# A four-layer vision kernel: one more filtered position in the second 3x3 convolution, middle outputs summed by accumulating transfers, one map buffer instead of two

## The chip, the cores and the metric

The kernel runs on one core of one Trainium2 chip. The metric is the device time of one execution in microseconds; every number here is from executions on the chip. A core has TensorE (PE, with its weight loads as PEld), VectorE (DVE), ScalarE (ACT), GpSimd (POOL), SyncE (SP), and 16 DMA engines that move data for queues which SP, ACT and POOL issue to.

## The reference

A tensor x of 4 images, 256 channels, 56 x 56, float32, passes four residual layers. Each normalizes x in 32 groups (`_gn`) and adds a branch:

```python
x = x + _L0_conv_ref(_gn(x), ...)   # involution 7x7, 16 groups
x = x + _L1_conv_ref(_gn(x), ...)   # two 3x3 convolutions
x = x + _L2_conv_ref(_gn(x), ...)   # involution 7x7 with batch norms
x = x + _L3_conv_ref(_gn(x), ...)   # spectral gates

def _L1_conv_ref(x, w1, g1, b1, rm1, rv1, w2, g2, b2, rm2, rv2):
    h = _conv3x3(x, w1, stride=1)
    h = jax.nn.relu(_bn(h, g1, b1, rm1, rv1))
    h = _bn(_conv3x3(h, w2, stride=1), g2, b2, rm2, rv2)
    return jax.nn.relu(x + h)
```

The change is in layer 1, the two 3x3 convolutions from 256 to 256 channels.

## The kernel before, in words

The layers run one after the other: the first involution up to about 517 us of the span, the convolution layer up to about 1166, then the second involution with the gates. Everything on an engine runs in the order in which the program emits it (`in_order` pins it), so a wait of one instruction holds all behind it on its engine.

`conv_layer` cuts each image into three chunks of rows, 12 chunks in all: 18, 20, 18 rows for the first convolution (`C1_ROWS`) and 16, 20, 20 for the second (`C2_ROWS`). The order is first 0, first 1, second 0, first 2, second 1, first 3, second 2, and so on; second 10 is followed by second 11. The output map of the first convolution is kept in `ph2`, which has two halves used in turn (`i % 2`).

Along a row both convolutions use a minimal-filtering transform: four outputs are computed from six products, the positions k, done in the order `KS = (1, 2, 3, 4, 0, 5)`. `transform` (L1414 to L1455, nine steps, VectorE, and one ACT copy of known rows, L1417) makes the six inputs v from a map; `input1` and `input2` are the two instances. VectorE then combines the six products into four outputs.

A position is done in one of two ways. *Unfiltered* (`unfiltered`, L1525): for each half `co` of the outputs, 6 products (3 rows x 2 halves of inputs) over the whole chunk. *Filtered* (`filtered_product`, L1540): a second transform along the column gives two outputs from four products over half the rows. For that it needs the columns' sums and differences of the input, `inner_columns` (L1491, L1492, VectorE) and `outer_columns` (ACT L1507, then an accumulating transfer by POOL, L1508), and transformed weights: the sum and the difference of three weight rows (`column_sums_of`, L1318 to L1320, VectorE) and scalings on ACT. Of a filtered position's four products, ACT copies the first from PSUM (L1549) and VectorE does three sums (L1550, L1551, L1553). Before the change, filtering is used for all six positions of first convolutions from chunk 2 on, five in chunk 1, none in chunk 0, and for positions 4 and 0 of all second convolutions. Each product of two float32 operands is two PE instructions in the trace.

PSUM is four tiles of two banks, used in turn (`two_banks`). A filtered position takes two tiles, an unfiltered one takes one.

Everything else is placed by hand into twelve lists `after[0]` to `after[11]` for every convolution: items of `after[2n]` are emitted inside the n-th position in `KS` order, those of `after[2n+1]` behind it. The text calls them slots. `place(after, g, at)` puts the steps of a generator g into the slots `at`. `late_r[k]` is a list for slot k of the *next* convolution (k of 12 and more is the one after that). `tail1` holds what the first convolution leaves to the next: the ACT passes `outputs` (L1570) that write `ph2`. `phases` (L1411, ACT) normalizes the next rows of x.

For chunks up to 9, `joined` hands the second convolution's outputs on: ACT writes the output scaled (L1652), a POOL transfer adds x (L1653), ACT applies the relu (L1660), a POOL transfer adds x again (L1661), SP stores the result (L1663), and ACT makes the sums for the next normalization (`mean_of` L1691, `spread_of` L1697, L1698). Chunks 10 and 11 load x (`load_residual`) and join on VectorE (L1670, L1675); chunk 10 adds x by a POOL transfer (L1685) and stores by POOL (L1686). `weights2` (`summed_weights`) forms the second convolution's weights by accumulating transfers from DRAM (L1298) during the first two chunks.

## Time and profile before

| | |
|---|---|
| median of 3 runs | 1714.48 us (1708.15 to 1714.85) |
| the profiled execution | 1717.23 us, its span 1715.5 us |
| busy, share of the span | PE 95%, PEld 85%, DVE 78%, ACT 58%, POOL 29% |
| L1525, unfiltered products | 1320 instructions, 295.1 us of PE |
| L1540, filtered products with all operands | 2848 instructions; the two largest groups 175.9 and 73.5 us |
| PE idle in the layer, largest waits | 7.6 us (a transfer into u_sb), 3.0 (DVE L1553), 2.9 (DVE L1608) |
| DMA queues, share of 16 engines | POOL's 24.8%, SP's 29.9% |

Busy times say how long an engine was executing; what an edit is worth follows from which engine ends last in the stage where it lies. Lengths of single matmuls overlap, so the cost of one is the distance between starts. An idle time in brackets stands before the instruction, with what ended it.

### The profile page before, as it was taken

The numbers are of one execution on the slowest core, as the hardware profiler recorded it, in microseconds if no ns is written. First come the engines' busy times: TensorE is split into PE (matmuls) and PEld (weight loads), VectorE is DVE, ScalarE is ACT, GpSimd is POOL, SyncE is SP. The second block draws the span as 40 slices with busy tenths as digits, with TensorE's granted clock in tenths as the row PEclk, the third lists the DMA queues.
The fourth block names the chain that finished last, engine by engine and source line by source line (L and its number), as shares of the span: only waits on it lengthen the run. The fifth ranks groups of instructions, "written<-read, shape, count | busy, mean of one in ns | idle before, by whom it ended". The sixth has DMA issues, their size and how long they took to land.

```text
span 1715.5 us, 57009 instructions
## 1 busy us (share of the span) xinstructions
PE 1632.9 (95%) x24488; PEld 1466.1 (85%) x24488; DVE 1333.8 (78%) x2439; ACT 1000.9 (58%) x2192; POOL 498.2 (29%) x711
## 2 busy tenths in 40 slices
PE   6999999999989999999999999988999999899988
PEld 4998998988987889899999889976988888788876
DVE  2687787777759998999889899947777778778775
ACT  1655556456545565565666456435667567577654
POOL 2124223322433222212212212110000572572571
PEclk9999999999999999999999999999999999999996
DMA  2354445433759666566766556644444765764762
GB/s 90 114 184 138 147 147 185 154 127 104 238 139 281 112 129 106 121 129 138 148 132 113 109 122 128 142 132 147 129 139 162 207 215 184 218 210 140 204 169 98
DMA packets 92490, 258.63 MB, mean 151 GB/s; under 512 B 14837, under 2 KB 37374, under 8 KB 88526
## 3 DMA queue, kind: packets, MB, share of 16 engines
q1 hardware_dynamic: 57438, 163.33, 29.9%
q0 software_dynamic: 33760, 90.37, 24.8%
q8 instruction: 194, 3.18, 0.8%
q10 hardware_dynamic: 1040, 1.26, 0.3%
q14 instruction: 58, 0.48, 0.1%
HBM read 95.07 MB, written 49.15 MB: 84 GB/s over the span
## 4 chain that ended last, share of the span: by engine, by line
PE 64%; DVE 15%; DMA 7%; issue 5%; ACT 3%; SPq 2%; POOL 2%; ACTq 0%; POOLq 0%; DVEq 0%
PE mm L1540 17%; PE ps L594 15%; PE ps L636 13%; PE mm L1525 11%; DVE kt L612 5%; DMA xw<-xw 4%; PE ps L408 3%; DVE un L656 3%; DMA u_sb<-in_wc_dram 2%; PE ps L470 1%; SPq L426 1%; SPq L427 1%; DVE st L1106 1%; ACT hp L489 1%; ACT xw L420 1%
## 5 line engine op out<-in xcount | busy, mean ns | idle before, releaser
L636 PE MATMUL ps<-kt,xw 126*32 126x48 f32 (+1 forms) x12544 | 381.7, 236 | 24.1 <-DMA xw<-xw 11.3
L636 PEld LDWEIGHTS ps<-kt,xw 126*32 126x32 f32 (+1 forms) x12544 | 343.0, 122 | 69.7 <-issue 44.0
L594 PE MATMUL ps<-hp,z_sb 64*126 64x133 f32 x6144 | 384.3, 279 | 9.0 <-DVE kt L612 4.9
L594 PEld LDWEIGHTS ps<-hp,z_sb 64*126 64x126 f32 x6144 | 364.4, 185 | 25.0 <-DVE kt L612 6.9
L612 DVE TENSOR_TENSOR kt<-ps,zb_sb 126x798 f32<-126x798 f32 x352 | 332.9, 980 | 59.3 <-PE ps L594 47.9
L605 ACT ACTIVATE kt<-ps,zb_sb 126x133 f32<-126x133 f32 x960 | 281.0, 442 | 107.3 <-PE ps L594 107.3
L1525 PE MATMUL mm<-v,u_sb 128*128 128x280 f32 (+2 forms) x1320 | 295.1, 383 | 1.7 <-DVE xs L1551 1.0
L1525 PEld LDWEIGHTS mm<-v,u_sb 128*128 128x128 f32 x1320 | 247.5, 189 | 41.8 <-issue 1.6
L1540 PE MATMUL mm<-xs,u_sb 128*128 128x126 f32 (+2 forms) x1392 | 175.9, 279 | 0.3 <-DVE xs L1551 0.3
L656 DVE SCALAR_TENSOR_TENSOR un<-ps,s,un 128x240 f32<-128x240 f32 x224 | 102.5, 457 | 89.0 <-ACT un L651 83.7
L1540 PEld LDWEIGHTS mm<-xs,u_sb 128*128 128x128 f32 x1392 | 168.5, 193 | 0.5 <-issue 0.5
L656 DVE SCALAR_TENSOR_TENSOR un<-ps,par_sb,un 128x240 f32<-128x240 f32 x224 | 97.6, 456 | 81.8 <-ACT un L649 77.9
L1508 POOL DMA_DIRECT2D xs<-v x82 | 75.2, 1006 | 285.3 <-ACT xs L1507 233.9
L661 POOL TENSOR_TENSOR xs<-un,xs 128x240 f32<-128x240 f32 x112 | 72.2, 665 | 216.3 <-DVE un L656 216.3
L420 ACT COPY xw<-ps 126x896 f32<-126x896 f32 x112 | 101.4, 906 | 39.0 <-PE ps L408 21.3
L649 ACT ACTIVATE un<-ps,par_sb 128x240 f32<-128x240 f32 x112 | 50.3, 449 | 119.1 <-PE ps L636 112.8
L151 POOL TENSOR_TENSOR norm_sb<-norm_sb,mhalf 128x1 f32<-128x1 f32 x32 | 19.8, 642 | 342.5 <-DVE norm_sb L150 342.5
L651 ACT ACTIVATE un<-ps,bn_t,s 128x240 f32<-128x240 f32 x112 | 60.1, 538 | 94.2 <-PE ps L636 86.0
L408 PE MATMUL ps<-ident_sb,strip_sb 128*126 128x128 f32 x784 | 110.6, 281 | 3.9 <-ACT hp L489 1.6
L408 PEld LDWEIGHTS ps<-ident_sb,strip_sb 128*126 128x126 f32 x784 | 84.0, 141 | 15.0 <-POOL strip_sb L393 4.6
L1411 ACT ACTIVATE ph<-xs,norm_sb 128x266 f32<-128x266 f32 (+2 forms) x96 | 80.4, 862 | 9.0 <-DMA xs<-x 7.3
L1540 PE MATMUL mm<-v_sb,u_sb 128*128 128x140 f32 (+2 forms) x536 | 73.5, 280 | 3.5 <-DVE xs L1553 3.0
(303 smaller groups left out, 2272.7 us busy)
## 6 DMA issues: line engine op xcount, KB each, us to landing
xw<-xw SPq DMA_DIRECT2D x224, 252.0 KB
xw<-xw SPq DMA_DIRECT2D x224, 126.0 KB
xs<-x POOLq DMA_DIRECT2D x26, 560.0 KB, 5.9
x<-xs POOLq DMA_DIRECT2D x8, 1568.0 KB, 7.8
xs<-x SPq DMA_DIRECT2D x8, 1568.0 KB
xs<-v POOLq DMA_DIRECT2D x42, 252.0 KB, 4.3
xs<-in_x_dram SPq DMA_DIRECT2D x6, 1568.0 KB
x<-xs SPq DMA_DIRECT2D x6, 1568.0 KB
```

Source lines behind the costliest of these rows:

```text
L408: nc.tensor.transpose(ps[:Q, k * P : (k + 1) * P], flat[:, k * Q : (k + 1) * Q], ident_sb)
L420: nc.scalar.copy(xw[:, :NSB, :], ps[:Q, : NSB * P].rearrange("q (n c) -> q n c", n=NSB))
L594: nc.tensor.matmul(ps[:Q, i, k * NT : (k + 1) * NT], z_sb[i * R : (i + 1) * R, cb * GB // 2 + gp, z0 : z0 + Q], hp[i * R : (i + 1) * R, py ...
L605: nc.scalar.activation(kt[:, g0 + i, pb, :, k], ps[:Q, i, k * NT : (k + 1) * NT], AF.Identity, bias=zb_sb[:, cb * GB + g0 + i, p0 + k : p0 ...
L612: nc.vector.tensor_tensor(kt[:, g0 : g0 + 2, pb], ps[:Q, :, : PB * NT].rearrange("q i (k t) -> q i t k", k=PB), zb_sb[:, cb * GB + g0 : cb ...
L636: nc.tensor.matmul(v[m * j : m * j + m, i, :, k * TP : (k + 1) * TP], xw[:, window(ty), m * j : m * j + m], kt[:, ng * j : ng * j + ng, :, ...
L656: nc.vector.scalar_tensor_tensor(part, o[e], s, part, ALU.mult, ALU.add)
L661: nc.gpsimd.tensor_tensor(dst, u, dst, ALU.add)
L1411: nc.scalar.activation(dst, xr[:, j], AF.Identity, bias=t, scale=s)
L1508: nc.gpsimd.dma_start(t[:, at], v[:, at], accum_op=ALU.add)
L1525: nc.tensor.matmul(ps, *position(u, v, ci, dy, k, co, n), start=(j == 0), stop=(j == NB * 3 - 1))
L1540: nc.tensor.matmul(ps[:, bank, co * m : (co + 1) * m], u[ci][:, co * P : (co + 1) * P], v2[:, : n // 2, ci * WT : (ci + 1) * WT], start=(c ...
```

## The change

- Second convolutions filter three positions, 3, 4 and 0, instead of 4 and 0; chunk 1 of the first convolution filters four (1 to 4) instead of five.
- The combination is rearranged. Before, positions 0 and 5 were folded in by scaled sums (`stt`) at the end. Now z and s, the first and the last output, are formed at position 4, and positions 0 and 5 are added onto them (`onto`), in `filtered_product` with a VectorE sum that broadcasts the first product in place of ACT's copy. The transform's sign at L1441 and the weights change with it.
- The two middle outputs get their last sum by `middle`: two POOL transfers that accumulate in SBUF and one ACT halving, in first convolutions from chunk 2 and second ones from 1 to 9; else two VectorE operations as before.
- `ph2` holds one chunk. All four `outputs` passes of a first convolution now stand in slots 0 to 3 of the following second convolution (except chunk 0). Of `input2`'s nine steps eight, not five, lie in the first convolution before. New room: `y_sb`, two more tiles for sums.
- Column sums of the weights used late (second convolution 3, 4, 0; first 0, 5) are made by `edge_column_weights`: ACT copies and scalings with three POOL transfers, for both input halves at once.
- Placement: the first L1652 pass of a chunk moves from the end of its convolution to slot 0 of the next, the second from slot 0 to slot 2; the relu and what follows one slot later. Outer columns of the second convolution stand in slots 0, 1, 2 (before 2 and 3), inner ones in 1 and 3. In the last chunk outer columns are made by one VectorE subtraction each. Chunk 10 stores by SP.

```diff
-                return KS[: (0, 5, 6)[min(i, 2)]]
+                return KS[: (0, 4, 6)[min(i, 2)]]
...
+                    nc.scalar.mul(us[ci][0], us[ci][0], 6.0)
...
-            FILTERED2 = (4, 0)
+            FILTERED2 = (3, 4, 0)
...
+            def edge_column_weights(u, k, x, scratch):
+
+                w0, w1, w2 = (u[:, :, y, k, :] for y in range(3))
+                s = y_tile(scratch)[:, : NB * C].rearrange("p (c n) -> p c n", c=NB)
+                nc.scalar.copy(s, w0)
+                nc.scalar.mul(x, w1, -1.0)
+                yield
+                nc.gpsimd.dma_start(s, w2, accum_op=ALU.add)
+                yield
+                nc.gpsimd.dma_start(x, s, accum_op=ALU.add)
+                nc.gpsimd.dma_start(w1, s, accum_op=ALU.add)
+                yield
+                for w, by in ((w1, 0.5), (x, 0.5), (w2, -1.0)):
                     nc.scalar.mul(w, w, by)
-
-            def filtered2(i):
-
-                return FILTERED2
+                yield
...
-            ph2 = wpool.tile([P, 4, 2 * PH_ROWS, NB, WT + 1], F32, name="ph2")
+            ph2 = wpool.tile([P, 4, PH_ROWS, NB, WT + 1], F32, name="ph2")
...
-                    stt(one(k), d, -4.0, far, ALU.mult, ALU.add)
+                    stt(one(k), d, 4.0, far, ALU.mult, ALU.subtract)
...
-                if (conv, i) == (1, 1):
+                if (conv, i) in ((1, 1), (2, n_chunks - 1)):
                     tt(t[:, at], v[:, at], v[:, below], ALU.subtract)
                 else:
                     nc.scalar.mul(t[:, at], v[:, below], -1.0)
...
-                nc.scalar.copy(o[:, 0], m1)
-                tt(o[:, 1], o[:, 0], m2, ALU.subtract)
-                tt(o[:, 0], o[:, 0], m2, ALU.add)
+                if onto is None:
+                    nc.scalar.copy(o0, m1)
+                    tt(o1, o0, m2, ALU.subtract)
+                else:
+                    tt(o, o, m1.to_broadcast([P, 2, NB * n // 2, WT]), ALU.add)
+                    tt(o1, o1, m2, ALU.subtract)
+                tt(o0, o0, m2, ALU.add)
                 run_all(items)
                 tt(o, o, outer[:, :, : NB * m].rearrange("p e (r t) -> p e r t", t=WT), ALU.add)
 
+            def middle(t, q, b, a, by_transfer):
+
+                if by_transfer:
+                    nc.gpsimd.dma_start(b, a, accum_op=ALU.add)
+                    nc.scalar.mul(t, t, 0.5)
+                    nc.gpsimd.dma_start(t, q, accum_op=ALU.add)
+                else:
+                    tt(b, b, a, ALU.add)
+                    stt(t, t, 0.5, q, ALU.mult, ALU.add)
...
                     elif k == 4:
                         tt(full(b), full(t), got, ALU.add)
                         tt(full(t), full(t), got, ALU.subtract)
-                        tt(b, b, a, ALU.subtract)
-                        stt(t, t, 0.5, q, ALU.mult, ALU.add)
-                    elif k == 0:
-                        stt(full(a), full(a), -0.75, got, ALU.mult, ALU.add)
-                        stt(a, b, 0.25, a, ALU.mult, ALU.add)
-                        outputs(2, 1)
-                    elif k == 5:
-                        stt(full(q), full(q), -3.0, got, ALU.mult, ALU.add)
-                        stt(q, t, 4.0, q, ALU.mult, ALU.add)
+                        stt(z, b, 0.25, a, ALU.mult, ALU.add)
+                        stt(s, t, 2.0, q, ALU.mult, ALU.add)
+                        middle(t, q, b, a, i > 1)
+                        if i == 0:
+                            edge_rows(i)
+                            outputs(2, 1)
                     run_all(after[2 * n_s + 1])
-                tail += [lambda: outputs(0), lambda: outputs(3)]
+                if i == 0:
+                    tail += [lambda: outputs(0), lambda: outputs(3)]
+                else:
+                    tail += [lambda: (edge_rows(i), outputs(0)), lambda: outputs(3), lambda: outputs(2), lambda: outputs(1)]
...
-                        if co == 0:
-                            leaves()
-                        else:
-                            late_r[0].append(leaves)
-                        k = 5 + 2 * co
+                        late_r[2 * co].append(leaves)
+                        k = 6 + 2 * co
...
-                        k = 10 + 2 * co
+                        k = 11 + 2 * co
...
-                    nc.gpsimd.dma_start(xout[bb][co][:, at], x)
+                    nc.sync.dma_start(xout[bb][co][:, at], x)
...
+                        middle(t, q, b, a, 0 < i and summed)
...
-                    stt(q[:, at], q[:, at], -3.0, ps, ALU.mult, ALU.add)
-                    stt(q[:, at], t[:, at], 4.0, q[:, at], ALU.mult, ALU.add)
+                    tt(s[:, at], s[:, at], ps, ALU.add)
...
-                        place(after, late_v, (1, 3, 5, 8, 10))
+                        place(after, late_v, (1, 3, 5, 6, 8, 9, 10, 11))
...
-                                after[0].append(lambda ci=ci: column_weights(ci, 0, 1))
-                                after[1].append(lambda ci=ci: filter_weights(ci, 0, 1))
+                            place(after, edge_column_weights(u2_sb, 3, ux2_sb[0], 6), (4, 5, 8, 11))
+                            fourth = edge_column_weights(u2_sb, 4, ux2_sb[1], 3)
+                            place(after, fourth, (5, 6, 9))
...
-                        place(after, late_v, (0, 0, 1, 1))
+                        place(after, late_v, (0,) if i < n_chunks - 1 else ())
...
+                    after[1].append(lambda i=i: inner_columns(2, i, 3, 4))
+                    after[3].append(lambda i=i: inner_columns(2, i, 0))
+                    for n, k in enumerate(FILTERED2):
+                        after[n].append(lambda i=i, k=k: outer_columns(2, i, k))
                     if i == 0:
...
+                        place(after, fourth, (1,))
+                        place(after, edge_column_weights(u2_sb, 0, ux2_sb[2], 5), (0, 1, 3, 5))
+                        place(after, edge_column_weights(u1_sb, 0, ux0_sb, 4), (3, 4, 6, 9))
+                        place(after, edge_column_weights(u1_sb, 5, ux5_sb, 5), (6, 7, 9, 11))
...
-                        place(after, input1(j), (1, 1, 2, 2, 3, 3, 4, 4, 5))
-                        columns_at(after, (6, 8), ((4, 1), (4, 2), (6, 3), (9, 4)), 1, j)
+                        place(after, input1(j), (1, 2, 2, 3, 3, 4, 5, 6, 7))
+                        columns_at(after, (6, 8, 11), ((4, 1), (5, 2), (7, 3), (9, 4)), 1, j)
                     elif nxt is not None:
-                        place(after, input2(nxt[1]), (1, 1, 2, 2, 3, 3, 4, 5, 6))
+                        place(after, input2(nxt[1]), (4, 4, 5, 5, 6, 6, 7, 8, 9))
```

## The prediction

> **What bounds the kernel now.** I read the page first: TensorE is busy 95% of the span, and its two convolution lines (L1525 unfiltered, L1540 filtered) lead the chain that ended last. Then the timeline of TensorE from one first convolution to the next, for the price of a position. "x24" or "x16" counts instructions; the difference of two starts is the real cost, since each length contains about 0.16 us of pipeline tail.
>
> ```profile
> 707.92 1.12 PE L1540 MATMUL mm<-v_sb,u_sb 128*128 128x140 f32 x8
> ...
> 711.73 5.82 PE L1525 MATMUL mm<-v,u_sb 128*128 128x280 f32 x24
> 717.39 1.12 PE L1540 MATMUL mm<-ph,u_sb 128*128 128x140 f32 x8
> ...
> 757.45 1.06 PE L1540 MATMUL mm<-v_sb,u_sb 128*128 128x112 f32 x8
> ...
> 761.02 4.72 PE L1525 MATMUL mm<-v,u_sb 128*128 128x224 f32 x24
> 765.58 1.05 PE L1540 MATMUL mm<-ph,u_sb 128*128 128x126 f32 x8
> ```
>
> A 20-row chunk pays 711.73-707.92 = 3.81 us for a filtered position and 717.39-711.73 = 5.66 for an unfiltered one: 1.85 saved by filtering. A 16-row chunk pays 3.57 and 4.56: 1.0 saved.
>
> Then the windows view, cut at chunk boundaries (first convolution, second, and again). Columns: length, busy PE, PEld, DVE, ACT, POOL, granted clock, DMA share, GB/s.
>
> ```profile
> 840.30:870.60 30.30, 30.30 (x162) 25.82 (x162) 28.87 (x46) 13.91 (x29) 5.25 (x6) 1.00 0.55 131
> 870.60:893.50 22.90, 22.90 (x194) 22.89 (x193) 18.90 (x35) 17.76 (x25) 5.39 (x8) 1.00 0.74 127
> 893.50:918.80 25.30, 25.30 (x163) 25.29 (x161) 24.79 (x38) 13.26 (x27) 5.22 (x6) 1.00 0.61 148
> ```
>
> TensorE never stops here, but VectorE is 95 to 98% busy in a second convolution (rows one and three) and 83% in a first. So time taken from TensorE comes back only if VectorE and what feeds it keep up.
>
> Last, the waits and the timelines where TensorE does stop: 7.6 us in the last chunk, behind POOL, and some 9 us of idle and slow clock around 555 to 570.
>
> ```profile
> 1151.91 4.07 PE L1540 MATMUL mm<-u_sb 128*128 128x140 f32 x16 [7.59 <-DMA u_sb<-v]
> ```
> ```profile
> 1139.44 0.57 POOL L1686 DMA_DIRECT2D x<-xs  x1 [5.22 <-DMA xs<-x]
> 1140.04 0.86 POOL L1685 DMA_DIRECT2D xs<-x  x1
> 1147.13 0.55 POOL L1686 DMA_DIRECT2D x<-xs  x1 [6.23 <-DMA xs<-x]
> 1147.67 1.76 POOL L1508 DMA_DIRECT2D u_sb<-v  x2
> ```
> ```profile
> 568.05 1.27 POOL L1298 DMA_DIRECT2D u_sb<-u_sb  x1 [0.78 <-DMA u_sb<-in_wc_dram]
> ```
>
> **The end: -12 us.** In the last chunk the outer columns went through ACT and a POOL transfer; POOL sat behind an output store (L1686) that waited for a landing. The change makes these columns on VectorE (0.73 each) and sends that store by SP, so the 7.6 goes. So does the slow clock after it: those 16 instructions took 4.07 where 2.07 is usual. VectorE is busy only 17.6 of this chunk's 40.5 us, so three columns and one more product hide there. Two chunks (10 and 11) save 1.85 each: 7.6+2.0+3.7 = 13.3. Chunk 10 gives back about 1.3: its middle sums stay on VectorE (+1.4) and the next chunk's nine transform steps (8.4 us) move from slots 1-6 to 4-9, behind products; VectorE then ends some 18 us of work against 17.1 of TensorE. Bounds -8 to -14; I take -12, near the plain sum, since the wait is shown. What is late next is VectorE's own tail.
>
> **The start (518 to 612): +4 us.** Removed from VectorE: column sums for first-conv positions 0, 5 and second-conv 4, 0 (24 operations of 0.43, 10 us), inner and outer columns of chunk 1's position 0 (2.0). Chunk 1 then loses its second wait (3.3) and the slow clock behind it (1.8), and pays 1.85 for position 0 unfiltered: its TensorE ends near 581, not 584. But the sums' first step is an ACT copy of position 3's weights at slot 4. Its last accumulation is issued at 568.05 and lands 7.7 later (median of L1298), at 575.8. ACT is in order: behind the copy stand phases (0.8 each), the copies of position 4 and that position's PSUM copy, which reaches VectorE near 580 instead of 568. VectorE then owes 13 us before the inner columns of the second convolution's position 3 exist (594, against TensorE's 590): 4 lost. Each later set of weights is a chain on POOL: ACT copy, transfer (4.3 to land), two transfers (1.0 to issue each, 4.3), three ACT scalings; position 0's is ready near 607, and I count 3 more. Chunk 0 would end near 616 against 612.3: +4. Bounds: -5 (weights early enough) to +10 (also each scaling blocks a PSUM copy and the clock drops).
>
> **The pairs between: -3 us.** TensorE saves 6x1.85+3x1.0 = 14. Per pair VectorE gets +1.6 (three operations of position 3's product), +0.9 (its inner columns), +2.2 (three broadcast sums in place of ACT copies), and loses 2.9+2.35 of scaled sums (L1604 to L1609, L1733 to L1742): -0.5 in all. The two middle sums it sheds are replaced by z and s. So its load stays, in a shorter pair: about 97%. POOL gets four sums and one outer column, 5x1.0; DMA engines 5x1.55 for 280 KB (the windows of 723 to 738 are filled for 15.4 us by the 2.8 MB of L1653, L1508 and L1661): 7.7 us more in 50, hidden, since their share is 0.55 to 0.74.
>
> Moved at no cost: the passes L1652 (2.45 each on ACT) from the end of the second convolution to slots 0 and 2 of the next first, where ACT is 17.8 of 22.9 us busy and gives up four output passes (2.2); the transforms of the next chunk, one slot later each; inner columns 0 and 5 (1.3) into the second convolution's last position, where VectorE else has 1 of 5.7 us. Without that cover each would cost its length. The single map is read last at slot 9 of the first convolution and rewritten from slot 0 of the second, so I expect no wait for it.
>
> What isn't hidden is order. (1) Three transform steps (3.2 us) move into the first convolution, so VectorE ends it 5 us late, not 3 to 4. (2) ACT: four output passes (1.1 each) and two means now stand at the start of the second. After the combinations (19 us into a 20-row first convolution, as L1602 ends now) come the halving on ACT 0.6, two POOL sums 2.0, then L1661, landing in 5.9: 26.5, or 3.6 into the second. Then, in order: mean 1.4, phases 0.75, outputs 1.1, outer column 0.5 (7.3), PSUM copy 0.45, mean 1.4, outputs 1.1, outer 0.5, row copy L1417 0.35 (11.1), outputs 1.1, outer 0.5, square 1.45, outputs 1.1 (15.2), and only then position 3's PSUM copy, which a 16-row chunk has ready at 11.0. L1417 holds VectorE's next transform until 11.1 in two chunks of three. From there VectorE has 17 us up to releasing the PSUM banks that the next first convolution needs: 28.0, where TensorE is done at 24.3 and the chunk takes 25.3 now: +2.7. The same count gives 30.25 against 30.3 for the 20-row chunk with L1417 and about -1.6 for the one without: +1.1 per image. With ACT never late, VectorE alone allows -4.7. The landing may be off by 2 us either way, so I take -1.0 per image, nearer to the count: -3. Bounds -14 and +15 (every chunk 1.2 us worse than counted, with cold clocks).
>
> The granted clock was 0.66 from 565 to 570, after waits of 2.9 and 3.0 us, and the 32 instructions there cost 1.8 us more. That is in the upper bound.
>
> The Trainium skill (TensorE: Matmul & The Clock Gate, "What's actually happening") says that an idle window of about 3.4 us halves the clock; by it the short new waits of 1 to 3 us cost nothing beyond themselves. This trace saw it dip after two shorter ones close together. By the trace's 1.8 us in each of nine chunks the sum would be 16 us worse, by the page none.
>
> The Trainium skill (DMA: Bandwidth & Descriptors, "Anatomy of one DMA") gives 2.0 us plus bytes at 436 GB/s, estimated 2.7 us for 280 KB; the row of L1508 has 4.7 for this accumulation. By the page each sum would land 2 us earlier, the pairs give about -8; the measurement decides.
>
> **Sum.** -12+4-3 = -11. The profiled execution took 1717.23 (span 1715.5, 1.7 around it), 2.7 above the median 1714.48 of three; the same -11 on the median gives 1703.5. 0.5%, 8.6 us, is what a measurement here can tell from none.
>
> **Rivals.** First: everything hides. Weights land in time (-3), ACT never holds VectorE (-14), the end as shown (-13): -30, 1684.5. For it: VectorE's total falls. Against: 97% load, and the means behind a landing.
>
> Second, slower: ACT's queue at the start of a second convolution decides. Each microsecond that position 3's PSUM copy comes later than counted costs each of nine chunks one; 1.2 later takes away the whole gain, 2.2 makes it slower by over 0.5%. At 2.7 later: -11+24 = +13, 1727.5. For it: position 3 is the second-convolution filter closest to the start. Against: ACT is only about half busy in second convolutions.
>
> **Numbers.** Forecast 0.5 (own range 1695 to 1712), first rival 0.25, second 0.25. Faster by over 0.5% (below 1705.9): 0.29 of the forecast's half and 0.24 of the first's, 0.53. Slower (above 1723): 0.19, from the second and its neighbourhood; within: 0.28. The range for 8 in 10 leaves out the outer tenth of each rival's side: 1683 to 1729.
>
> **What would show it.** Right: no wait on u_sb<-v in the last chunk; a second convolution of 16 rows at least as long as 25.3 us, VectorE waiting there for ACT's L1417 or position 3's PSUM copy; ACT waiting for a landing near 565 to 576. The first rival: 20-row pairs near 49.9 us with no TensorE wait. The second: waits of 3 us or more in every second convolution. Wrong altogether: new TensorE waits on transfers, or a changed later layer.

## The result and the profile after

The changed kernel takes 1761.26 us, the median of 4 runs (1757.48 to 1772.66), against 1714.66 before in the same session: a ratio of 1.0285, 95% interval 1.0256 to 1.0314, clearly slower. The forecast was 1703.5 with a range up to 1729. The profiled execution took 1757.48, its span 1755.7; before, 1717.23 and 1715.5.

The layer can be cut into the prediction's three steps, with what lies behind it as a fourth (us; distances between starts of products in the traces). A pair is a first convolution and the second convolution behind it:

| | before | after | predicted | measured |
|---|---|---|---|---|
| start: first product to first convolution 2 | 93.6 | 97.9 | +4 | +4.3 |
| pairs: from there to second convolution 10 | 482.2 | 524.6 | -3 | **+42.4** |
| end: from there to the layer's last product | 71.2 | 65.1 | -12 | -6.1 |
| later layers | 549.7 | 549.7 | 0 | 0.0 |

So one term is wrong by 45 us and one by half. Here are windows of the profile after, the same three chunks that the prediction showed (second convolution 5, first 7, second 6; length, then busy PE, PEld, DVE, ACT, POOL, granted clock, DMA share, GB/s):

```profile
862.37:895.97 33.60, 30.34 (x171) 26.79 (x170) 25.57 (x42) 17.92 (x35) 7.38 (x13) 0.95 0.69 155
895.97:918.89 22.92, 22.92 (x193) 22.92 (x192) 20.70 (x40) 14.37 (x17) 7.98 (x11) 1.00 0.79 136
918.89:951.60 32.71, 27.50 (x171) 27.34 (x170) 24.72 (x42) 16.83 (x35) 7.88 (x10) 0.90 0.71 157
```

The first convolution is unchanged (22.9). The second ones, which should have become shorter, take 33.6 and 32.7 us where they took 30.3 and 25.3. TensorE stops in them, and VectorE is no longer full: 24.7 of 32.7 us, where it was 24.8 of 25.3. Neither is the bound; something holds both. TensorE's timeline in the same chunks says where it stops:

```profile
879.02 3.39 PE L1549 MATMUL mm<-xs,u_sb 128*128 128x140 f32 x16 [3.26 <-DMA xs<-v]
...
935.12 3.73 PE L1549 MATMUL mm<-xs,u_sb 128*128 128x112 f32 x16 [5.21 <-DMA xs<-v]
```

These are the products of position 3's outer column, which ACT's L1516 and POOL's transfer L1517 make (L1507 and L1508 before). They wait for its landing, and the 16 instructions behind then last 3.4 to 3.7 us instead of 2.0: the clock, 0.95 and 0.90 in the windows. The Trainium skill (TensorE: Matmul & The Clock Gate, "What's actually happening") puts the clock's fall at an idle window of about 3.4 us; six waits of 3.26 to 5.81 us here, each with such slow products behind it, agree roughly.

From the list of waits of the profile after, three lines (total, times, longest):

```profile
ACT xs L1709 <- DMA xs<-x: 45.3, 9, 6.0
DVE v L1449 <- ACT v L1425: 29.5, 10, 7.8
PE mm L1549 <- DMA xs<-v: 29.3, 8, 5.8
```

ACT's L1709, the mean of a finished chunk, waits for the second accumulation of x (L1681, L1661 before). ACT runs in order, so behind it stand position 3's outer column, whose lateness stops TensorE, and the known rows L1425, which stop VectorE. Of the eight waits in the third line six are long, 3.3 to 5.8 us, in second convolutions 1, 2, 3, 5, 6 and 8; the other two are 0.67 and 0.25. In those six the mean starts 6.0 to 7.8 us into the chunk. In 4 and 7 it starts after 3.6, and TensorE doesn't wait for the column. The timelines of POOL, SP, ACT, POOL and PE around second convolution 2 (its start is 695.73) show one such chain:

```profile
691.80 0.86 POOL L1572 DMA_DIRECT2D hp<-y_sb  x1 [7.19 <-DVE hp L1623]
693.05 0.86 POOL L1574 DMA_DIRECT2D hp<-xs  x1 [0.39 <-ACT hp L1573]
693.59 1.21 POOL L1681 DMA_DIRECT2D xs<-x  x1
693.57 11.55 SPq L1165 DMA_DIRECT2D xs<-x  x2
702.54 1.14 ACT L1709 ACTIVATE xs<-xs 128x1120 f32<-128x1120 f32 x1 [5.48 <-DMA xs<-x]
705.66 0.65 ACT L1516 ACTIVATE xs<-v 128x560 f32<-128x560 f32 x1
706.61 0.86 POOL L1517 DMA_DIRECT2D xs<-v  x1 [9.88 <-ACT xs L1516]
713.01 3.56 PE L1549 MATMUL mm<-xs,u_sb 128*128 128x140 f32 x16 [3.89 <-DMA xs<-v]
```

L1681 stands in POOL's queue behind the two new middle sums (L1572, L1574), and SP's load of the next rows (L1165) starts beside it. It lands 9.0 us after its issue, 6.8 into the second convolution. The trace's answer for this line says the same of the whole layer. Before (L1661), this is who waited for it, and its landing:

```profile
  ACT xs L1691: 0.2, 1
...
DMA to landing us min/median/max: 5.3/6.6/8.3
```

and after (L1681):

```profile
  ACT xs L1709: 45.3, 9
...
DMA to landing us min/median/max: 6.2/8.9/10.6
```

The end after: no wait on u_sb<-v is left, as predicted, but second convolution 10 begins with a wait, and three more follow around its end, each on VectorE:

```profile
1140.79 11.56 PE L1534 MATMUL mm<-v,u_sb 128*128 128x280 f32 x48 [1.84 <-DVE hp L1565]
...
1171.80 0.35 PE L230 MATMUL mm<-d,gavg_sb 128*128 128x1 f32 x2 [1.65 <-DVE hp L1565]
1172.97 0.38 PE L230 MATMUL mm<-d,gavg_sb 128*128 128x1 f32 x2 [0.82 <-DVE hp L1567]
1173.95 14.62 PE L1534 MATMUL mm<-v,u_sb 128*128 128x280 f32 x48 [0.60 <-DVE hp L1757]
```

48 unfiltered instructions usually take 11.5; here 14.62 after waits of 1.65, 0.82 and 0.60, none of which is near 3.4 us.

### The profile page after: what moved, and what is told of

It is laid out like the page before. It is cut to its first block, busy times and chain, and to the rows that moved or that the text cites. A ratio compares the mean times of both kernels' runs of the same rounds, so it can differ in the third digit from the quotient of the medians.

```text
span 1755.7 us, 57351 instructions
## 1 busy us (share of the span) xinstructions
PE 1634.9 (93%) x24576; PEld 1471.6 (84%) x24576; DVE 1316.1 (75%) x2422; ACT 1006.4 (57%) x2188; POOL 555.6 (32%) x771
## 4 chain that ended last, share of the span: by engine, by line
PE 53%; DVE 19%; DMA 12%; issue 7%; ACT 6%; POOL 2%; SPq 1%; ACTq 0%; POOLq 0%; DVEq 0%
PE ps L636 15%; PE ps L594 14%; PE mm L1549 12%; DVE kt L612 5%; DMA xs<-x 4%; PE mm L1534 4%; PE ps L408 3%; DVE un L656 3%; DMA xs<-v 2%; DMA xw<-xw 2%; DMA u_sb<-in_wc_dram 2%; PE ps L470 2%; DVE hp L1567 1%; DVE st L1106 1%; ACT ph L1592 1%
## 5 line engine op out<-in xcount | busy, mean ns | idle before, releaser
L636 PE MATMUL ps<-kt,xw 126*32 126x48 f32 (+1 forms) x12544 | 379.8, 235 | 24.8 <-issue 13.6
L636 PEld LDWEIGHTS ps<-kt,xw 126*32 126x32 f32 (+1 forms) x12544 | 341.9, 121 | 69.8 <-issue 46.1
L594 PEld LDWEIGHTS ps<-hp,z_sb 64*126 64x126 f32 x6144 | 365.5, 186 | 24.7 <-DVE kt L612 7.4
L1534 PE MATMUL mm<-v,u_sb 128*128 128x280 f32 (+2 forms) x1056 | 242.2, 388 | 7.2 <-DVE hp L1565 5.5
L1549 PE MATMUL mm<-xs,u_sb 128*128 128x140 f32 (+2 forms) x1552 | 206.5, 288 | 32.3 <-DMA xs<-v 29.3
L1534 PEld LDWEIGHTS mm<-v,u_sb 128*128 128x128 f32 x1056 | 200.7, 192 | 41.4 <-issue 6.3
L1549 PEld LDWEIGHTS mm<-xs,u_sb 128*128 128x128 f32 x1552 | 196.5, 200 | 34.3 <-issue 29.8
L1517 POOL DMA_DIRECT2D xs<-v x93 | 93.7, 1068 | 170.9 <-ACT xs L1516 122.8
L1549 PE MATMUL mm<-v_sb,u_sb 128*128 128x140 f32 (+2 forms) x624 | 87.9, 285 | 6.7 <-DVE hp L1565 2.7
L1549 PEld LDWEIGHTS mm<-v_sb,u_sb 128*128 128x128 f32 x624 | 81.4, 196 | 9.0 <-ACT u_sb L1349 2.7
```

The costliest lines, as they stand in the source:

```text
L594: nc.tensor.matmul(ps[:Q, i, k * NT : (k + 1) * NT], z_sb[i * R : (i + 1) * R, cb * GB // 2 + gp, z0 : z0 + Q], hp[i * R : (i + 1) * R, py ...
L636: nc.tensor.matmul(v[m * j : m * j + m, i, :, k * TP : (k + 1) * TP], xw[:, window(ty), m * j : m * j + m], kt[:, ng * j : ng * j + ng, :, ...
L1517: nc.gpsimd.dma_start(t[:, at], v[:, at], accum_op=ALU.add)
L1534: nc.tensor.matmul(ps, *position(u, v, ci, dy, k, co, n), start=(j == 0), stop=(j == NB * 3 - 1))
L1549: nc.tensor.matmul(ps[:, bank, co * m : (co + 1) * m], u[ci][:, co * P : (co + 1) * P], v2[:, : n // 2, ci * WT : (ci + 1) * WT], start=(c ...
```

## The experiments

Theory 1: ACT, held at L1709, makes position 3's outer column late. Theory 2: VectorE is the bound, whatever ACT does. Theory 3: the DMA engines are too full (POOL's queue moved 56.0 MB between 600 and 1140 us, before 43.1; the 41.9 of the first expectation is its count up to 1100). "Pairs" is the second row of the table above, from the one profile of each kernel. Each ratio is to runs of the kernel before in the same session, whose medians went from 1711 to 1717.

| kernel | us | ratio to before, 95% interval | pairs |
|---|---|---|---|
| before | | | 482.2 |
| after | 1761.26 | 1.0285 (1.0256 to 1.0314) | 524.6 |
| e1 means late | 1726.16 | 1.0064 (1.0034 to 1.0093) | 484.8 |
| e2 row loads late | 1756.85 | 1.0233 (1.0200 to 1.0266) | 514.7 |
| e3 no middle transfers | 1751.56 | 1.0211 (1.0192 to 1.0229) | 510.0 |
| e4 outer column by VectorE | 1742.96 | 1.0175 (1.0135 to 1.0214) | 506.6 |
| e5 two positions | 1727.26 | 1.0083 (1.0054 to 1.0112) | 503.4 |
| e6 means late, mended | 1722.77 | 1.0062 (1.0032 to 1.0092) | 483.5 |
| e7 and norm's steps early | 1714.42 | 0.9991 (0.9977 to 1.0006) | 471.6 |
| e8 and start, transforms | 1710.38 | 0.9976 (0.9949 to 1.0003) | 479.5 |
| e9 and weights spread | 1702.03 | 0.9942 (0.9919 to 0.9964) | 476.4 |
| e10 e4 and known rows by VectorE | 1741.14 | 1.0169 (1.0131 to 1.0208) | 500.7 |
| e11 before, end alone | 1704.79 | 0.9955 (0.9937 to 0.9973) | 482.2 |
| e12 e7 with two positions | 1707.24 | 0.9963 (0.9944 to 0.9983) | 479.2 |
| e13 second sums ahead of the middle | 1733.89 | 1.0098 (1.0069 to 1.0127) | 486.1 |
| e14 e9, 128 instructions more | 1709.74 | 0.9954 (0.9931 to 0.9977) | 477.7 |
| e15 e9, 256 more | 1740.17 | 1.0134 (1.0112 to 1.0156) | 477.2 |
| e16 e9, 128 more, cheap | 1692.67 | 0.9893 (0.9871 to 0.9916) | 476.9 |

### Who holds ACT: the means later

```diff
-                        k = 11 + 2 * co
+                        k = 15 + 2 * co
```

> The two means (L1709) and squares of a finished chunk go four slots later, behind the outer column of position 3 in ACT's queue. Theory 1 (ACT stands in front of the landing of the second accumulation, so position 3's outer column is late): the eight TensorE waits on it, 29.3 us in the changed kernel, shrink to under 8, and the slow clock behind them (8 x 1.5 to 2 us) mostly goes: 1761 - 21 - 12 = 1728 us, 1718 to 1738. Theory 2 (VectorE, nearly full, is the bound whatever ACT does): the wait moves to VectorE, 1761, 1754 to 1768. Theory 3 (the DMA engines are too full: 56.0 instead of 41.9 MB on POOL's queue between 600 and 1140): the column is issued 5 us earlier but lands as late under load, 1755, 1748 to 1764.

1726.16. The waits on the landing are gone from ACT's list, TensorE's on transfers fall from 29.3 to 2.5 us, VectorE's for L1425 from 29.5 to 12.6, and the pairs give back 40 of their 42 us:

```profile
PE mm L1549 <- DMA xs<-v: 2.5, 2, 1.4
```

The landing itself is as late as before the edit (9.3 in the next run): nobody waits for it now. In this run the stores of chunk 9 slid past the refill of their buffer, so those rows of the output are not its own; the next one keeps the last image's stores in place (`k = (15 if bb < B - 1 else 11) + 2 * co`).

> As the first experiment (means and squares four slots later), but the last image, which has no means, keeps its stores where they were. The waits say the same as there: 1726, 1720 to 1732.

1722.77: theory 1 holds. Theories 2 and 3 fall as accounts of the 42 us, since no byte and no VectorE work went.

### Why the landing is late

The row loads, from slot 11 of a first convolution to slot 4 of the second behind it:

```diff
-                            if i + 2 < n_chunks:
-                                after[11].append(lambda i=i: load_rows(i + 2, xin))
...
+                    if i + 3 < n_chunks:
+                        after[4].append(lambda i=i: load_rows(i + 3, xin))
```

> The load of the rows of the chunk after next goes from the last slot of a first convolution to slot 4 of the second convolution behind it, so it no longer runs beside the second accumulations. Theory 1 with collision as its cause: their landing falls from 9.0 us to about 6 (5.9 before the change), ACT's wait L1709 from 45.3 to under 20 us, TensorE's from 29.3 to under 8: 1732 us, 1720 to 1742. Theory 1 with POOL's queue order as its cause: the landing stays over 8, 1759, 1754 to 1765. Theory 2 (VectorE bound): 1761, 1754 to 1768. Theory 3 (too many bytes on the DMA engines): the collision only moves, 1760, 1752 to 1768.

1756.85. The landing falls to 7.1, ACT's wait to 32.0, TensorE's to 19.3: the collision is real, but a small part of it. The Trainium skill (DMA: Bandwidth & Descriptors, "Issuing engines are not separate DMA queues") says that transfers of different issuing engines share the same 16 DMA engines and interleave. The 1.8 us by which POOL's sum lands sooner without SP's load beside it agree.

The middle sums back on VectorE:

```diff
-                        middle(t, q, b, a, i > 1)
+                        middle(t, q, b, a, False)
...
-                        middle(t, q, b, a, 0 < i and summed)
+                        middle(t, q, b, a, False)
```

> The two middle sums of every chunk (L1572 to L1574: two POOL transfers and a halving on ACT) go back to VectorE as one addition and one scaled addition; nothing else changes. Theory 1 with POOL's queue as the cause of the late landing: the second accumulation (L1681) lands after 6 to 7 us instead of 9.0, ACT's wait at L1709 falls from 45 to some 20 us, TensorE's from 29.3 to under 10; VectorE has 2 x 1.45 more per pair, of which half shows: 1761 - 28 + 13 = 1746, 1735 to 1755. Theory 2 (VectorE is the bound): 2.9 x 9 more, 1761 + 26 = 1787, at least 1775.

1751.56, between the two. The landing falls to 6.7, ACT's wait to 15.8, no TensorE wait on a transfer is left in the list; but VectorE, with some 2.9 us more per pair, now stops TensorE (16.9 us before L1549 and 8.2 before L1534, on L1565). This takes away bytes and order at once, so the next one changes the order alone: the second ReLU and sum one slot earlier, the first of them ahead of the middle sums in POOL's queue.

```diff
-                        k = 6 + 2 * co
+                        k = 5 + 2 * co
```

> The changed kernel with the second ReLU and accumulation (L1680, L1681) one slot earlier, so that the first of them stands in POOL's queue ahead of the two middle sums (L1572, L1574) instead of behind them; the means stay where the change put them, and no transfer and no byte goes. If the order in POOL's queue made it late: it is issued some 4 us earlier and lands after 7 instead of 8.9 us, ACT's wait at L1709 falls from 45 to under 12 us, TensorE's on transfers from 29 to under 8, and the time to that of the late means, 1727, 1720 to 1735. If the bytes on the DMA engines did: it lands as late under the same load, 1752, 1745 to 1760.

1733.89, and the pairs 486.1. In the same place as above, L1681 is now issued at 687.33 instead of 693.59:

```profile
687.33 0.86 POOL L1681 DMA_DIRECT2D xs<-x  x1 [2.12 <-ACT xs L1680]
692.51 0.86 POOL L1572 DMA_DIRECT2D hp<-y_sb  x1 [4.32 <-DVE hp L1623]
```

ACT's wait is 6.0 us in place of 45.3, and the landing is only little shorter:

```profile
ACT xs L1709 <- DMA xs<-x: 6.0, 6, 1.3
...
DMA to landing us min/median/max: 6.7/8.0/9.3
```

Every byte is still moved. So the load lengthens the landing (6.7 without the middle sums, 7.1 without the row loads beside it, 8.0 here), and the place in POOL's queue decides whether an engine stands waiting for it. The pairs give 38.5 us. The time gives 27; in this profile the start took 2.9 us longer, the later layers 10.7 and those ahead 5.

### The arms behind ACT

The outer column of position 3 by one VectorE subtraction, and then the known rows L1425 by VectorE too:

```diff
-                if (conv, i) in ((1, 1), (2, n_chunks - 1)):
+                if (conv, i) in ((1, 1), (2, n_chunks - 1)) or (conv, k) == (2, 3):
```
```diff
-                    nc.scalar.copy(
+                    nc.vector.tensor_copy(
                         v[:, :, : known * NB].rearrange("p k r t -> p k (r t)"),
```

> Position 3's outer column of every second convolution is made by one VectorE subtraction (0.6 to 0.75 us) in place of ACT's pass and POOL's transfer; nothing else changes. Theory 1: no TensorE wait on a transfer there (29.3 us) and no slow clock behind it (some 14), +0.7 us of VectorE in each of nine chunks in part on the path: 1761 - 43 + 6 = 1724 us, 1715 to 1735. Theory 2 (VectorE bound): slower by the added work, 1761 + 7 = 1768. Theory 3 (DMA engines): 2.5 of 56 MB less, 1756, 1750 to 1762.

> The changed kernel with position 3's outer column on VectorE, as in an experiment before (1743), and the copy of known rows L1425 moved from ACT to VectorE as well (0.4 to 0.6 us in two chunks of three, for each convolution). Two arms (ACT held by the mean holds TensorE by the outer column and VectorE by L1425, 26.3 us of waits in that run): the second arm goes too, 1743 - 16 = 1727, 1720 to 1735, about what the late means gave. Rival (VectorE's load, so that any work added to it costs): 1743 + 8 = 1751, at least 1743.

1742.96 and 1741.14: the first arm was worth 18 of the 37 us expected, the second 2 of 16. ACT's wait stayed at 45 us in both, and each thing taken out from behind it left another in its place: first position 4's outer column (TensorE 8.4 us) and L1565 (14.0), then the PSUM copy of position 3 (VectorE's waits for L1560 rise from 23.8 to 31.7). In these two runs the held engine had to be freed, not its customers.

### Two positions

```diff
-            FILTERED2 = (3, 4, 0)
+            FILTERED2 = (4, 0)
```

(and position 3's weights and inner columns taken out)

> Position 3 of the second convolution stays unfiltered (its column sums, inner and outer columns fall away); sums by transfers, one map and the late weights by transfers stay as in the changed kernel. TensorE gets back 14 us in the pairs and 3.7 at the end, and the first filtered position starts 5.7 (20 rows) or 4.6 us later. Theory 1: the waits of 29.3 and the slow clock of 14 go almost wholly since position 4's outer column has that much more time; 1761 - 43 + 18 = 1736 us, 1725 to 1745. Theory 2 (VectorE): 2.5 us less of its work per chunk makes up for the TensorE time, and the rest is the bound: 1750, 1745 to 1765. Theory 3: 1755.

1727.26, lower than any theory's figure and within theory 1's range. The first filtered position starts one position later, so of ACT's wait of 50.5 us only 2.2 reaches TensorE by the outer column. But with as many filtered positions as before the change the pairs are still 21 us longer. What ACT holds now is VectorE (L1425, 33.6 us), and TensorE waits for VectorE's L1565, 7.5 us before L1549 and 6.6 before L1534.

### The ring of PSUM tiles

With the means late, two pairs still took 57.1 us. TensorE at the start of the first of them, second convolution 4 of e1:

```profile
788.89 0.51 PE L219 MATMUL mm<-mv,gavg_sb 128*128 128x1 f32 x4
791.24 13.24 PE L1534 MATMUL mm<-v,u_sb 128*128 128x280 f32 x48 [1.84 <-DVE hp L1565]
```

L219 belongs to the next norm. Its two small products take two tiles of the same ring of four, so the next position needs a tile earlier than else, while VectorE still reads it. If so, steps of the norm placed elsewhere take the wait away:

```diff
                 for g in slow:
-                    after[5].append(step(g))
-                    after[11].append(step(g))
+                    place(after, g, (0, 1, 3) if conv == 2 else ())
```

> The run before, and the steps of the next norm (L212 to L235, two small products in PSUM buffers of the same ring of four) go from slots 5 and 11 of every chunk to slots 0, 1 and 3 of second convolutions. With the means late, two pairs (the second convolutions 4 and 7) still took 57.1 us against 52.9 before the change, and each began with a wait of 1.84 on VectorE's L1565 behind such a product. Theory 4 (the extra buffer of the norm's product moves the ring by one, so TensorE needs a buffer that VectorE, some us behind, still reads; then the slow clock): 5 us less in each of the second convolutions 4, 7 and 10: 1726 - 14 = 1712, 1706 to 1718. Rival (VectorE is that far behind in these chunks anyway): 1726, 1720 to 1730.

1714.42. The waits of 1.84 are gone. The pairs give 11.9 and the end 3.4 (63.9 to 60.5), about the sum that was expected; the time gives 8.3, and in this profile the later layers took 4 us longer.

### Start and transforms

Position 3 is left unfiltered in second convolution 0, its weights are made one chunk later, and six of nine transform steps stand one slot earlier:

```diff
-                return FILTERED2
+                return FILTERED2 if i else FILTERED2[1:]
...
-                            place(after, edge_column_weights(u2_sb, 3, ux2_sb[0], 6), (4, 5, 8, 11))
-                            place(after, fourth, (5, 6, 9))
+                            place(after, fourth, (8, 9, 11))
+                        if j == 1:
+                            place(after, edge_column_weights(u2_sb, 3, ux2_sb[0], 6), (0, 1, 3, 5))
...
-                        place(after, input1(j), (1, 2, 2, 3, 3, 4, 5, 6, 7))
+                        place(after, input1(j), (1, 2, 2, 2, 2, 3, 4, 5, 6))
```

> The run before, and two more: position 3 stays unfiltered in the second convolution 0 alone, its column sums are made one chunk later and position 4's begin four slots later (ACT's first copy held ACT for 9.7 us behind a landing at 575); and two transform steps of the next first convolution go from slots 3 to 5 into slot 2, where VectorE stood 6.7 us behind position 2's product. If the start's +4 comes from ACT held by that copy: 612 instead of 616 at the end of chunk 0 or earlier, -4; the steps another -0.5 a pair, -4: 1712 - 8 = 1704, 1695 to 1712. Rival (POOL's weights chain is the start's limit, and VectorE's idle time there is not on the path): 1712, 1707 to 1716.

1710.38, between the two. The start falls from 99.3 to 89.6 us, but the first pair rises to 62.4, by the same kind of stall, an ACT instruction that waits for a landing (ACT, then TensorE):

```profile
632.39 0.63 ACT L1349 ACTIVATE u_sb<-u_sb 128x512 f32<-128x512 f32 x1 [9.10 <-DMA u_sb<-y_sb]
636.10 2.04 PE L1549 MATMUL mm<-v_sb,u_sb 128*128 128x126 f32 x8 [7.29 <-DVE hp L1565]
```

So these weights' steps were spread over slots 2, 4, 7, 11.

> The run with all edits, but position 3's column sums are spread over slots 2, 4, 7 and 11 of the first convolution 2 instead of 0, 1, 3 and 5. There ACT stood 9.1 us at L1349 behind the landing of L1346, TensorE 7.3 behind VectorE's L1565, and the first pair took 62.4 us against some 50 later. If that stall is what ate the start's gain: 1710 - 12 = 1698, 1692 to 1705, which would be faster than before the change (1715). Rival (the transfers of these weights are the limit wherever ACT waits for them): 1708, 1705 to 1714.

1702.03, 0.6% below before. But the reason that was expected did not come: the first pair is still 60.2, since L1349 still holds ACT, for 8.4 us, and the stall now stands at position 3's column in second convolution 1:

```profile
654.88 4.10 PE L1549 MATMUL mm<-xs,u_sb 128*128 128x140 f32 x16 [4.91 <-DMA xs<-v]
```

The pairs are 3.1 us shorter than e8's; the later layers, whose code is the same, were 7.7 shorter in this profile, and those ahead 5 longer. The other pairs stand at 50.0 to 50.3 (20 rows) and 47.2 to 48.2 (16 rows), where before had 51.7 to 52.9 and 48.2. For 20 rows that is 1.7 to 2.6 less, the prediction's 1.85 or more. In their second convolutions (5, 6 and 9 here) TensorE stops for 0.7 us or not at all, although VectorE is busy 91 to 99% of the time:

```profile
842.87:871.74 28.87, 28.87 (x174) 25.50 (x173) 26.31 (x45) 16.14 (x32) 7.86 (x13) 1.00 0.78 183
894.62:919.84 25.22, 24.56 (x170) 24.40 (x169) 24.36 (x42) 16.08 (x33) 7.12 (x10) 1.00 0.88 204
1043.38:1067.71 24.33, 24.33 (x170) 24.32 (x169) 23.99 (x42) 15.21 (x33) 6.28 (x10) 1.00 0.76 160
```

### One part alone, and the price of a position

The last chunk's outer columns by VectorE and its predecessor's store by SP, in the kernel before:

```diff
-                if (conv, i) == (1, 1):
+                if (conv, i) in ((1, 1), (2, n_chunks - 1)):
...
-                    nc.gpsimd.dma_start(xout[bb][co][:, at], x)
+                    nc.sync.dma_start(xout[bb][co][:, at], x)
```

> One part alone: the kernel before the change, with the last chunk's outer columns by VectorE's subtraction and the last finished rows stored by SP's queue in place of POOL's. The prediction's reading: the 7.6 us wait on u_sb<-v and the 2.0 of slow clock behind it go, 1715 - 9.6 = 1705, 1702 to 1709. Rival (another wait, on VectorE, takes its place): 1713, 1710 to 1716.

1704.79: the wait of 7.6 and its slow clock are worth about what the profile said (the end 71.2 to 61.2). The 8.9 us by which the time fell are no separate proof: in this profile, the fastest of twelve runs, other stages whose code is as before were 8 us shorter too.

And e7 with position 3 unfiltered again:

> The ordered version of the changed kernel (means late, norm's steps early: 1714) with position 3 of the second convolution unfiltered again. Theory 1 (with the queues in order TensorE is the bound, so a filtered position pays its 1.0 to 1.85 us in each of eleven chunks, and its weights cost some 4 at the start): 1714 + 18 - 4 = 1728, 1722 to 1733. Theory 2 (VectorE is the bound): position 3's operations are saved and TensorE's time hides, 1712, 1705 to 1716.

1707.24, against theory 1's sum. It is lower than e7's time, but the intervals of the two ratios overlap (0.9944 to 0.9983, 0.9977 to 1.0006), and the stages say why it is no plain verdict: e12's 20-row pairs take 51.7 to 52.8 us, e7's 49.9 to 51.5, so the position pays there; its 16-row pairs are 48.2, e7's 47.6 to 49.1, so there it pays nothing (in e9, 0 to 1.0); and e7's later layers take 557.4 us in its profile, e12's 545.5. The layer itself is 4.4 us shorter with three positions, the time 7 us longer.

### What the later layers lose

The later layers' code is the same in all kernels. In the list of waits, TensorE's at L636 for "issue" (nothing that the profile shows) are 7.3 us before, 19.2 in e9, 3.9 in e12. One or two of these us lie in the first involution. The changed kernel has 49,152 matmuls and weight loads and 194 transfers of 16 KB on an instruction queue, 253 each if all of these bring TensorE's. So the guess was that the place of the stream in such blocks matters. To move the stream, products of one column stand ahead of the layer:

```diff
+            for _ in range(32):
+                nc.tensor.matmul(ps[:, :1], ident_sb, room["rows"][:, :1], start=True, stop=True)
```

(64 of them in e15; in e16 the three warming products are replaced by 35 with 32 weight columns)

> The best version with 32 products of one column ahead of the convolution layer, where TensorE is idle: 128 more instructions in TensorE's stream, half of one of the 16 KB transfers on the instruction queue. If the place of the stream in these blocks sets the waits for issue at L636 in the later layers (19.2 us against 7.3 before the change): they change by over 6 us, and the time by as much, 1694 or 1710. If not: 1702, 1698 to 1706, and 16 to 22 us of such waits.

> The control of the run before: 64 such products, 256 instructions, a whole block. By either account the time and the waits at L636 stay: 1702, 1698 to 1706, 16 to 22 us.

> The best version with the three warming products (L1799, 4.8 us) ahead of the convolution layer replaced by 35 products of 32 weight columns and one column, so TensorE's stream moves by 128 instructions, half a block. If the place in the blocks sets what the later layers lose: waits for issue at L636 under 10 us and 1695, 1688 to 1700, unless the small products last over 5 us. If the later layers' length is not tied to it: 1702, 1698 to 1707, more if the first products then run on a slow clock.

1709.74, 1740.17, 1692.67. TensorE wasn't idle there: the products of e14 and e15 lay on the path with 10.55 and 24.82 us. But the waits followed the half block. They are, in one profile each of e9, e14, e15 and e16:

```profile
PE ps L636 <- issue: 19.2, 17, 2.5
```
```profile
PE ps L636 <- issue: 6.2, 7, 2.7
```
```profile
PE ps L636 <- issue: 21.4, 15, 3.3
```
```profile
PE ps L636 <- issue: 5.5, 8, 1.3
```

In e16 the products cost 3.90 us in place of 4.78, and it has the best time, 1.07% below before. How much of that the shift gave is not shown. TensorE's waits at the same line for transfers of xw rise from 6.7 us (e9) to 12.4 (e16) as the others fall, so both together fall by 8.0. The later layers took 552.5 (e9), 548.9, 563.6 and 545.8 us: e9 and e15 differ by 11 us with like waits for issue, so these don't account for the lengths alone. And the layers ahead, which none of these edits touches, ended 3.9 us sooner in e16's profile than in e9's (515.5 and 519.4; 514.6 before). What sets these lengths stays open.

## Why the prediction was wrong, by its own steps

**Start, +4: right in size, its parts in part.** +4.3. ACT stood 9.7 us at the copy L1340 until 575.3, as foreseen. Chunk 1 gave 1.5 us where 3 were counted, and chunk 0 took 5.9 longer where 7 were counted. The 4 us at position 3 did not come: TensorE waited there 1.0 in all, then 2.3 for position 4's outer column, which was not counted, and 2.5 for position 0's weights, with slow products behind. That the sum hits so closely is in part luck.

**End, -12: the mechanism right, the size half.** -6.1. The 7.6 wait went, and in e11, alone, it brought 10.0. What failed is the 1.3 given back by chunk 10: the norm's products stood in the ring of PSUM tiles at that point, which the prediction didn't price. They brought 1.84 us of wait at the start and slow products at the tail (14.62 us instead of 11.5). With the means late and these products moved the end is 60.5, -10.7.

**Pairs, -3: wrong by 45.** Two steps failed. First, "L1661, landing in 5.9: 26.5, or 3.6 into the second". The issue came where that sentence has it: 26.5 - 5.9 is 2.3 us ahead of a 16-row second convolution, and the trace has 2.3 in three such chunks. (The terms as listed, 19 + 0.6 + 2.0 + 5.9, add up to 27.5; the trace bears out the 26.5.) The landing is the term that was too small. The median over the whole run was 6.6 already and became 8.9, so in the 16-row chunks the mean started 6.9, 6.0 and 4.5 us in. The 7.7 us of DMA time per pair were called hidden because the engines' share was 0.55 to 0.74: a mean share says nothing on the one transfer that an in-order engine stands behind.

Second, the prediction listed position 3's outer column in ACT's queue and never worked out when its transfer would land. By its own figures that is, as an estimate, 12.0 us into a 16-row chunk (7.3 on ACT, then the 4.7 that it gives for such an accumulation), where TensorE comes to it at 10.9 (two unfiltered positions of 4.56 and half of 3.57). Even with the landing as counted there was about 1 us to lose in such a chunk; with the landing late TensorE waited 5.8 and 5.2 us in two of the three.

The second rival had the mechanism, a late queue of ACT at the start of second convolutions, and asked for waits of 3 us or more in every one; they came in six of nine. Its price, one microsecond in each of nine chunks for each that ACT is late, gives 29 for the 3.2 us of second convolution 2, and TensorE's listed waits are 29.3; but they are six waits of 3.3 to 5.8 us, so that agreement is luck. It named the wrong customer: TensorE was stopped by position 3's outer column, earlier in ACT's queue than the PSUM copy that it named. Behind each long wait the 16 instructions took 1.3 to 2.0 us more, some 13 in six chunks with what followed. TensorE's own 14 us were saved all the same, so the loss to explain is 42.4 + 14 = 56: 29 of waits, 13 of slow products, and the 12 that e7 took from the ring of PSUM tiles make 54.

**VectorE "about 97%"** was right as a load and did not bind. In the changed kernel its share in the two second convolutions shown above fell to three quarters, since it was held too; in e9 it is 91 to 99%, and TensorE hardly stops beside it.

**The first rival, all hidden (-30, 1684.5),** is reached by two thirds in the layer once the queues are in order: e16 has the start -4.8, the pairs -5.3 (with the first pair at 59.9 instead of 53.4) and the end -10.7. But e16 also leaves position 3 of second convolution 0 unfiltered and has other edits than the change, so it doesn't show that rival for the change itself.

## What to carry to other kernels

An in-order engine's wait is paid by everything behind it: before moving work or adding transfers, go through each queue and ask what stands in front of the next landing, and place reads of a landing (means, copies, scalings of weights) as late as their users allow. When a transfer is added to a queue, count its effect on every later transfer of that queue, and how many slots their readers have to spare; here one slot of order gave back 38 of the pairs' 42 us with every byte kept. Taking single customers out from behind a held engine gave 18 and 2 us, freeing the engine 38. And when a step is moved, look at where its stall goes: spreading the weights' steps moved it by one convolution and gave 3 us, and the rest of that run's gain lay in layers that were not touched.

## What the runs showed of the hardware

- Waits shorter than 3.4 us slowed TensorE in some places and not in others: where 11.5 us is usual for 48 instructions, they took 13.24 after a wait of 1.84 behind the norm's products (e1), 11.56 after the like wait behind the like products (the changed kernel, 1140.79), and 14.62 after waits of 1.65, 0.82 and 0.60. What decides between these is not shown.
- TensorE's waits for issue at one line of the involutions changed from 19.2 us to 6.2 and 5.5 when its stream moved by 128 instructions, and to 21.4 when it moved by 256, in one profile each.
- Accumulating transfers within the chip (224 to 280 KB, the middle sums) landed after medians of 3.1 to 3.8 us, and those of the first convolutions that met SP's row loads (L1574, issued within 0.6 us of them) after 6.0 to 7.0; with the row loads moved (e2) the same ones landed after 3.6 to 5.0.
